# A Mamba block with a quantized feed-forward: the first sequence transposed and partly convolved on TensorE, and new places for the work at both ends

## The chip, the cores and the metric

The kernel runs on one core of a Trainium2 chip. The metric is device time in microseconds (us) of one execution; lower is better. The median of three runs of the kernel before is 1844.12 us (1842.97 to 1844.41).

A core has five engines, each with its own instruction queue worked off in order: PE (TensorE, matrix products), DVE (VectorE) and ACT (ScalarE) for elementwise work, POOL (GpSimd) for elementwise work too, and SP (SyncE), which here only issues DMAs. Engines wait for each other by semaphores. A waiting instruction holds up everything behind it in its own queue.

## The reference

Eight sequences of 2048 tokens with 256 features pass through a Mamba-like mixer and a feed-forward layer whose operands are rounded to FP4. Cut to what matters:

```
xz = x @ W_in;  x_proj, z = split(xz)          # 512 channels each
xc = causal_conv4(x_proj) + conv_b             # per channel, 4 taps
x_conv = silu(xc)
ssm = x_conv @ W_xproj                         # 1 + 16 + 16 columns
delta = softplus(ssm[0]);  Bm = ssm[1:17];  Cm = ssm[17:33]
h_mean = sum over the whole sequence of x_conv * (delta * Bm) / L
y = h_mean * Cm + D * x_conv
x = layernorm(x + (y * silu(z)) @ W_out)
g = fp4(x) @ fp4(w_gate).T;  u = fp4(x) @ fp4(w_up).T
x = layernorm(x + fp4(silu(g) * u) @ fp4(w_down).T)
```

`h_mean` is a sum over all tokens of a sequence: nothing after it can start for a sequence before its last token has passed the convolution and the softplus. `fp4` scales each block of 16 values by its maximum and rounds.

## The kernel before, in words

**Tiles.** A sequence is cut into 4 blocks of 512 tokens (32 blocks in all, named b0 to b31 here), and each block into 2 pairs of 256 tokens (64 pairs). The 512 channels are 4 chunks (c) of 128 partitions.

**Block, first half (`begin_block`, lines 575 to 754).** Channels lie on partitions, tokens along the row. Per chunk: `project` (PE, L602), `fetch` copies the result from PSUM (ACT, L611), `halo` copies the three last tokens of the block before (POOL, L595 and L597), `first` is the first tap (ACT, L616), three `tap`s follow (DVE, L622), then `silu` (ACT, L628). Then `x_projection` (PE, L635), `keep_ssm` (ACT, L645) and `by_token` (DVE, L650). To bring tokens onto the partitions, every chunk is `split` into 16-bit halves (ACT, L664), turned by a DMA transpose (issued by SP, L670) and put together again by `turned` (ACT, L678). `weigh` (DVE, L688) forms the delta column from it, `softplus` follows on DVE with one power on POOL (L502 to L526, L505), `delta_b` (DVE, L654) writes the tile `dB`, and `sums` (PE, L702) adds the block to the running sum. After a sequence's fourth block, `mean` (L712), `spread_mean` (L716) and `keep_mean` (L722) give `hT`.

**Block, second half (`mix_block`).** `state` (PE, L766) and `mix` (DVE, L777) form y, four blocks later (`LAG = 4`).

**Pair (`finish_pair`).** `zed` (PE, L810), `silu_z` (ACT, L821), `gated` (POOL, L826), `out` (PE, L833), `residual1` (DVE, L843), layernorm (DVE L545, POOL L551 to L556, ACT L559), the rounding q1 (DVE L289 to L328, ACT L320), whose result goes through a DMA transpose and is scaled by POOL (L392, tile `xqT`), `gate` and `up` (PE, L856), `silu_g` (ACT, L874), `product` (DVE, L881), the rounding q2 in the same way (tile `hqT`), `down` (PE, L887), `residual2` (DVE, L896), a second layernorm, `store`. The very last pair is worked in two halves of 128 tokens and transposes on PE (`finish_last`, L952 to L1043).

**Weights.** `w_gate`, `w_up` and `w_down` are rounded and transposed at the start in five portions (`prepare_...`): a load, the same rounding on DVE, ACT and POOL, transposes on PE (L451, L424, L487) and copies by ACT.

**The order of the work** is written out by hand. Every piece is put in a list with a place, a number; the list is sorted by it and the instructions are issued in that order, on each engine's queue:

```
    def at(base, table, name, index, f, *args):
        events.append((base + place, len(events), f, args))
```

For block n the base is n * 64, for its second half and its pairs (n + 4) * 64. The places come from the tables `BLOCK`, `PAIR`, `LAST` and `PREPARE`, the same for all blocks and pairs. Buffers come from rotating pools; PSUM has seven banks for all products and one for the running sum.

Of the kernel before, what the change touches and what calls it, by code (L numbers as in the profile page):

```python
# [8 lines left out]
F32 = mybir.dt.float32  # L9
BF16 = mybir.dt.bfloat16  # L10
U16 = mybir.dt.uint16
AF = mybir.ActivationFunctionType
ALU = mybir.AluOpType
# [3 lines left out]
P = 128  # L17
# [2 lines left out]

SIXTH = 0.16666668653488159
LN_EPS = 1e-5

# [2 lines left out]
PERIOD = 64.0  # L28
LAG = 4
BLOCK = {  # L30
    "load": -64.24,
    "halo": (-56.64, 17.17, 44.94, 44.05),
    "project": (-6.65, 11.59, 35.63, 20.08),
    "fetch": (1.54, 22.24, 57.11, 39.62),
    "first": (31.29, 32.95, 58.72, 51.03),
    "tap": ((35.31, 59.00, 62.56), (65.55, 67.78, 68.04), (72.08, 76.04, 76.92), (68.69, 69.87, 71.31)),
    "silu": (66.68, 70.49, 81.23, 75.04),
    "skip": (93.43, 94.37, 91.85, 154.42),
# [59 lines left out]
    "q1_gather_scales": (116.45, 146.97),  # L98
    "q2_gather_scales": (173.72, 195.66),
}  # L100
LAST = {
    "out": (101.01, 124.29),
    "residual1": (191.05, 124.61),
    "n1_stats": (194.16, 124.76),
    "n1_rstd": (197.81, 154.90),
    "n1_apply": ((198.21,), (173.78,)),
    "q1_scales": (212.63, 186.63),
    "q1_normalize": (212.96, 190.36),
    "q1_magnify": (213.66, 197.40),
    "q1_add": (229.95, 199.27),  # L110
    "q1_subtract": (370.03, 201.46),
    "q1_scale": (381.67, 203.71),
    "turn_xq": (512.71, 208.03),
    "turned_xq": (555.93, 212.80),
    "gate_up": ((593.00, 642.64, 617.68), (428.82, 267.08, 393.51)),
    "silu_g": ((596.51, 688.55, 679.34), (441.86, 473.75, 424.74)),
    "product": ((640.93, 768.07, 698.95), (535.88, 574.29, 531.93)),
    "q2_scales": (807.40, 593.68),
    "q2_normalize": (887.88, 627.15),
    "q2_magnify": (914.06, 635.31),  # L120
    "q2_add": (968.66, 643.81),
    "q2_subtract": (1012.32, 644.76),
    "q2_scale": (1095.84, 763.77),
    "turn_h": ((1144.78, 1139.10), (796.35, 946.12)),
    "turned_h": ((1205.14, 1146.35), (869.55, 1017.90)),
    "down": (1276.90, 1047.48),
    "residual2": (1296.41, 1121.36),
    "n2_stats": (1401.69, 1155.25),
    "n2_rstd": (1486.43, 1223.57),
    "n2_apply": ((1522.05,), (1243.96,)),  # L130
    "store": (1640.76, 1326.67),
}
PREPARE = {
    "weights": 27.56,
    "load": (-121.97, 130.79, 184.98, 271.53, 340.39),
    "scales": (-20.38, 135.83, 201.49, 277.18, 344.23),
    "normalize": (-15.59, 137.98, 203.68, 281.65, 345.11),
    "magnify": (17.95, 144.61, 207.82, 281.80, 360.53),
    "add": (31.07, 148.24, 209.79, 282.31, 368.84),
    "subtract": (96.60, 150.57, 211.47, 295.54, 376.69),  # L140
    "scale": (106.05, 151.39, 216.10, 314.72, 378.29),
    "turn": ((113.97,), (167.73, 177.76, 171.02), (249.86, 266.74, 247.22), (330.75, 339.14, 315.56, 339.84), (381.85, 389.94, 381.25, 386.21)),
}

@with_exitstack
def mamba_fp4_ffn_kernel(
# [16 lines left out]
    nc = tc.nc  # L163
    B, L, DM = x.shape
# [13 lines left out]
    NF = FF // P  # L178
    TAIL = FF - NF * P
    G = 32  # L180

    xf = x.rearrange("b (i t p) d -> b i p t d", p=P, t=NT)
    xTf = x_t.rearrange("b (k p) l -> b p k l", p=P)
# [41 lines left out]
    nc.vector.tensor_reduce(place, ident.rearrange("p (j n) -> p n j", n=G), AX.X, ALU.add)  # L225
    spread = const.tile([P, TT, G], F32, name="spread")
    nc.vector.tensor_copy(spread, place.unsqueeze(1).to_broadcast([P, TT, G]))
    nc.sync.dma_start(w_in_sb[:, :, :DI], w_in[:, :DI].rearrange("(k p) n -> p k n", p=P))

    xpool = ctx.enter_context(tc.tile_pool(name="xpool", bufs=2))  # L230
    keep = ctx.enter_context(tc.tile_pool(name="keep", bufs=LAG + 2))
# [2 lines left out]
    small = ctx.enter_context(tc.tile_pool(name="small", bufs=4))  # L234
    fp4 = ctx.enter_context(tc.tile_pool(name="fp4", bufs=2))

    def load_weights():
        nc.sync.dma_start(cw_sb, conv_w.rearrange("(c p) o k -> p c (o k)", p=P))
        nc.sync.dma_start(cb_sb, conv_b)
        wx = w_xproj.rearrange("(c p) n -> p c n", p=P)  # L240
        nc.sync.dma_start(w_xp_sb[:, :, :DS], wx[:, :, 1 + DS :])
        nc.sync.dma_start(w_xp_sb[:, :, DS:], wx[:, :, 1 : 1 + DS])
        nc.sync.dma_start(w_delta_sb, w_delta.to_broadcast([P, DI]))
        nc.sync.dma_start(w_in_sb[:, :, DI:], w_in[:, DI:].rearrange("(k p) n -> p k n", p=P))
        nc.sync.dma_start(dk_sb, d_skip)
        nc.sync.dma_start(w_out_sb, w_out.rearrange("(c p) n -> p c n", p=P))
# [3 lines left out]
    def at(base, table, name, index, f, *args):  # L250
        place = table[name]
        for i in index:
            place = place[i]
        events.append((base + place, len(events), f, args))

    def bank():
        return ps.tile([P, 512], F32, tag="ps", name="ps")
# [316 lines left out]

    def begin_block(n):

        b, i = divmod(n, NBLK)
        s = tiles["block", n] = {}

        def at_piece(name, f, *args):  # L580
            at(n * PERIOD, BLOCK, name, args, f, *args)

        def load():
            s["xT"] = xpool.tile([P, KM, T], F32, tag="xT", name="xT")
# [35 lines left out]
        def tap(c, k):  # L620
# [2 lines left out]
                acc, xp[:, k + 1 : k + 1 + T], cw_sb[:, c, k + 1 : k + 2], acc, ALU.mult, ALU.add  # L623
            )

        def silu(c):
            acc = s["xc"][:, c, :]
            nc.scalar.activation(acc, acc, AF.Silu, bias=cb_sb[:, c : c + 1])  # L628

        def x_projection():  # L630

# [15 lines left out]
        def by_token():  # L647

            s["ssm"] = p2.tile([P, P], F32, tag="ssm", name="ssm")
            nc.vector.transpose(s["ssm"], s["ct"])  # L650
            s["delta"] = small.tile([P, TT], F32, tag="delta", name="delta")

        def delta_b():
            nc.vector.tensor_tensor(  # L654
# [20 lines left out]
        def turned(c):  # L675
# [6 lines left out]
                s.pop(("hwT", c)).rearrange("p h t n -> p t n h"),  # L682
            )

        def weigh(t):
            if "d" not in s:
                s["d"] = small.tile([P, TT], F32, tag="d", name="d")
            nc.vector.scalar_tensor_tensor(  # L688
                p2.tile([P, DI], BF16, tag="xd", name="xd", bufs=1),
                s["xct"][:, t, :],  # L690
                1.0,
                w_delta_sb,
                ALU.mult,
                ALU.mult,
                accum_out=s["d"][:, t : t + 1],
            )

        def sums():
            if i == 0:
                hsum_of[b] = ps_h.tile([P, DI], F32, tag="h", name="hsum")  # L700
            for t in range(TT):
                nc.tensor.matmul(  # L702
                    hsum_of[b][t * G : (t + 1) * G, :],
                    dB_of[n % 2][:, t, :],
                    s["xct"][:, t, :],
                    start=(i == 0),
                    stop=(i == NBLK - 1),
                )
# [21 lines left out]
        for c in range(NC):  # L730
            at_piece("halo", halo, c)
            at_piece("project", project, c)
            at_piece("fetch", fetch, c)
            at_piece("first", first, c)
            for k in range(KC - 1):
                at_piece("tap", tap, c, k)
            at_piece("silu", silu, c)
            at_piece("skip", skip, c)
        at_piece("x_projection", x_projection)
        at_piece("keep_ssm", keep_ssm)  # L740
        at_piece("by_token", by_token)
        for c in range(NC):
            at_piece("split", split, c)
            at_piece("turn", turn, c)
            at_piece("turned", turned, c)
        for t in range(TT):
            at_piece("weigh", weigh, t)
        softplus(at_piece, lambda: s["d"], lambda: s["delta"])
        at_piece("delta_b", delta_b)
        at_piece("sums", sums)  # L750
        if i == NBLK - 1:
# [4 lines left out]
    def mix_block(n):  # L756

        b = n // NBLK
        s = tiles["block", n]

        def state():
            s["y"] = [bank().rearrange("p (c n) -> p c n", n=P) for _ in range(TT)]
            for c in range(NC):
                for t in range(TT):
                    g = slice(t * G, t * G + DS)
                    nc.tensor.matmul(  # L766
                        s["y"][t][:, c, :],
                        hT_of[b][g, c * P : (c + 1) * P],
                        s["ct"][g, :],
                        start=True,  # L770
                        stop=True,
                    )

        def mix(g):
            xc = s["xc"].rearrange("p c (t g r) -> p g c t r", g=TT, r=G)[:, g]
            y = s["y"][g].rearrange("p c (t r) -> p c t r", r=G)
            nc.vector.tensor_tensor(xc, xc, y, ALU.add)  # L777

        at((n + LAG) * PERIOD, BLOCK, "state", (), state)
        for t in range(TT):  # L780
            at((n + LAG) * PERIOD, BLOCK, "mix", (t,), mix, t)

    def finish_pair(m):

# [3 lines left out]
        s = tiles["block", n]  # L788
        q = {}

        def at_piece(name, f, *args):
            at((n + LAG) * PERIOD, PAIR, name, (half,) + args, f, *args)

        def stage(prefix):
            return lambda name, f, *args: at_piece(prefix + name, f, *args)
# [107 lines left out]
        for j in range(NC // 2):  # L903
            at_piece("zed", zed, j)
            at_piece("silu_z", silu_z, j)
            at_piece("gated", gated, j)
        if m == B * L // U - 1:
            for t in range(NT):
                finish_last(m, t, s, q)
            return  # L910
# [25 lines left out]
    def finish_last(m, t, s, pair):  # L936
# [129 lines left out]
        layernorm(stage("n2_"), x1, 1)  # L1066
        at_piece("store", store)

    at(0.0, PREPARE, "weights", (), load_weights)
    for n in range(B * NBLK):  # L1070
        begin_block(n)
# [61 lines left out]
```

## Time and profile before

| | |
|---|---|
| median of 3 runs | 1844.12 us |
| the profiled execution | 1842.3 us, span 1840.5 us |
| mean granted TensorE clock | 0.982 |
| PE busy | 1761.9 us (96% of the span) |
| DVE, ACT, POOL busy | 1551.0, 1021.5, 789.6 us |
| DMA | 203.62 MB, mean 111 GB/s |

The span is from the first to the last instruction; 1.8 us of the execution lie around it. "Busy" of PE counts the time in which a matmul runs. The granted clock is the share of full speed that the throttle gave TensorE. A float32 matmul leaves two records in the trace, a transpose by PE leaves one: a `project` (two matmuls) shows as four records.

A timeline row gives the start, the length, the engine, the line, the tiles and the count of a group of instructions, and in brackets the idle time of the engine before it with what ended that idle time. A row by stages gives the busy time (and count) of each engine in a stretch of the span, and the granted clock.

### The profile page before, as it was taken

What the parts mean: (1) busy time and instruction counts of PE and PEld (TensorE: products, weight loads), DVE (VectorE), ACT (ScalarE), POOL (GpSimd) and SP (SyncE); (2) the same over time, 40 slices, a digit from 0 to 9 for tenths busy, and PEclk for the clock granted to TensorE, in tenths of its full rate; (3) what the DMA queues carried; (4) which work ended last, traced back from release to release, by engine and by line L of the source; (5) the groups of instructions that cost most, each with busy time, mean ns of one, the idle gap of its engine ahead of it and who ended that gap; (6) DMA issues with size and microseconds to landing.
All of it is one profiled execution on the core that took longest, in us unless ns stands there. A gap on an engine that the chain in (4) does not pass through costs nothing.

```text
span 1840.5 us, 27813 instructions
## 1 busy us (share of the span) xinstructions
PE 1761.9 (96%) x9550; PEld 1407.9 (76%) x9550; DVE 1551.0 (84%) x3087; ACT 1021.5 (56%) x1554; POOL 789.6 (43%) x962
## 2 busy tenths in 40 slices
PE   5579999999999999999999999999999999999986
PEld 2246778888787888778788878788887878888874
DVE  4879989888888988888888888898888889877774
ACT  6886655556555555655555555555566556433222
POOL 1114353544434354453445444444444443455553
PEclk8799999999999999999999999999999999999997
DMA  4344664554555545555555555555455554444431
GB/s 128 89 102 90 118 124 110 114 124 104 121 121 112 118 115 121 104 122 121 112 115 120 114 108 125 122 113 118 116 112 114 121 114 103 121 106 102 99 85 27
DMA packets 383549, 203.62 MB, mean 111 GB/s; under 512 B 307120, under 2 KB 358192, under 8 KB 383408
## 3 DMA queue, kind: packets, MB, share of 16 engines
q1 hardware_dynamic: 383408, 201.85, 49.9%
q8 instruction: 75, 1.23, 0.3%
q14 instruction: 66, 0.54, 0.1%
HBM read 116.34 MB, written 20.91 MB: 75 GB/s over the span
## 4 chain that ended last, share of the span: by engine, by line
PE 87%; DVE 6%; issue 2%; POOL 2%; DMA 2%; ACT 1%; SPq 0%; POOLq 0%; DVEq 0%; ACTq 0%
PE ps L856 31%; PE ps L887 17%; PE ps L833 11%; PE ps L810 11%; PE ps L602 10%; PE ps L766 2%; PE hsum L702 2%; PE ps L635 1%; DVE xc L622 1%; DMA hwT<-hw 1%; DMA q_gT<-q_w 1%; DVE q_amax L289 1%; DMA xT<-in_x_t_dram 1%; POOL hqT L392 0%; DVE xd L688 0%
## 5 line engine op out<-in xcount | busy, mean ns | idle before, releaser
L887 PE MATMUL ps<-wdT,hqT 128*128 128x256 f32 x1512 | 342.4, 383 | 14.4 <-POOL hqT L392 14.4
L887 PEld LDWEIGHTS ps<-wdT,hqT 128*128 128x128 f32 x1512 | 286.9, 191 | 76.1 <-issue 22.6
L856 PE MATMUL ps<-wgT,xqT 128*128 128x256 f32 (+1 forms) x1512 | 328.6, 364 | 0.9 <-POOL xqT L392 0.9
L856 PE MATMUL ps<-wuT,xqT 128*128 128x256 f32 (+1 forms) x1512 | 320.2, 361 | 0.1
L856 PEld LDWEIGHTS ps<-wuT,xqT 128*128 128x128 f32 x1512 | 274.8, 190 | 50.2 <-issue 13.2
L856 PEld LDWEIGHTS ps<-wgT,xqT 128*128 128x128 f32 x1512 | 272.3, 190 | 45.7 <-issue 14.1
L826 POOL TENSOR_TENSOR xc<-xc,sz 128x512 f32<-128x512 f32 x128 | 162.6, 1281 | 298.5 <-DVE xc L777 263.7
L622 DVE SCALAR_TENSOR_TENSOR xc<-xp,cw_sb,xc 128x512 f32<-128x512 f32 x384 | 280.1, 750 | 5.8 <-ACT xc L616 1.7
L392 POOL TENSOR_TENSOR hqT<-q_gT,hqT 128x1408 f32<-128x1408 bf16 x63 | 185.6, 2947 | 207.2 <-PE ps L856 124.4
L821 ACT ACTIVATE sz<-ps 128x512 f32<-128x512 f32 x128 | 72.7, 595 | 335.3 <-PE ps L810 335.3
L602 PE MATMUL ps<-xT,w_in_sb 128*128 128x512 f32 x512 | 250.7, 616 | 8.5 <-DMA xT<-in_x_t_dram 8.5
L810 PE MATMUL ps<-xTz,w_in_sb 128*128 128x256 f32 x1024 | 241.8, 380 | 0.0
L833 PE MATMUL ps<-w_out_sb,xc 128*128 128x256 f32 x1008 | 231.0, 382 | 0.5 <-POOL xc L826 0.5
L810 PEld LDWEIGHTS ps<-xTz,w_in_sb 128*128 128x128 f32 x1024 | 195.3, 191 | 39.0 <-issue 13.8
L881 DVE TENSOR_TENSOR h<-sg,ps 128x512 f32<-128x512 f32 (+1 forms) x189 | 120.8, 640 | 116.0 <-PE ps L856 116.0
L874 ACT ACTIVATE sg<-ps 128x512 f32<-128x512 f32 x189 | 102.6, 560 | 203.6 <-PE ps L856 203.4
L833 PEld LDWEIGHTS ps<-w_out_sb,xc 128*128 128x128 f32 x1008 | 189.0, 190 | 31.3 <-POOL hqT L392 4.8
L320 ACT ACTIVATE q_w<-q_x 128x512 bf16<-128x512 f32 (+3 forms) x131 | 130.1, 993 | 94.5 <-DVE q_x L312 94.4
L324 DVE SCALAR_TENSOR_TENSOR q_x<-q_w,q_x 128x512 f32<-128x512 bf16 (+3 forms) x131 | 151.4, 1156 | 17.6 <-ACT q_w L320 15.0
L602 PEld LDWEIGHTS ps<-xT,w_in_sb 128*128 128x128 f32 x512 | 99.7, 199 | 86.6 <-issue 81.7
L559 ACT ACTIVATE x<-x,ln_nb,ln_rs 128x256 f32<-128x256 f32 x256 | 142.4, 595 | 31.4 <-POOL ln_nb L556 31.2
L328 DVE SCALAR_TENSOR_TENSOR q_w<-q_w,q_x 128x512 bf16<-128x512 bf16 (+3 forms) x131 | 151.6, 1158 | 2.4
(114 smaller groups left out, 2305.0 us busy)
## 6 DMA issues: line engine op xcount, KB each, us to landing
hqT<-q_rows SPq DMA_DIRECT2D x63, 704.0 KB
xT<-in_x_t_dram SPq DMA_DIRECT2D x32, 512.0 KB
xTz<-in_x_t_dram SPq DMA_DIRECT2D x64, 256.0 KB
xt<-in_L_attn_x_dram SPq DMA_DIRECT2D x64, 256.0 KB
xqT<-q_rows SPq DMA_DIRECT2D x63, 256.0 KB
out_dram<-x SPq DMA_DIRECT2D x63, 256.0 KB
q_rows<-q_scT SPq DMA_DIRECT2D x252, 4.0 KB
q_rows<-q_scT SPq DMA_DIRECT2D x252, 12.0 KB
```

The lines of the kernel that those rows point to most:

```text
L320: nc.scalar.activation(state["g"], state["x"], AF.Abs, scale=GRID)
L324: nc.vector.scalar_tensor_tensor(xn, w, 1.5 * GRID, xn, ALU.max, ALU.subtract)
L328: nc.vector.scalar_tensor_tensor(w, w, 1.5 * GRID, xn, ALU.max, ALU.subtract)
L392: nc.gpsimd.tensor_tensor(qT(), state["gT"], qT(), ALU.mult)
L559: nc.scalar.activation(r()[:, t, :], r()[:, t, :], AF.Identity, bias=v["nb"][:, t : t + 1], scale=v["rstd"][:, t : t + 1],)
L602: nc.tensor.matmul(mm, w_in_sb[:, k, c * P : (c + 1) * P], s["xT"][:, k, :], start=(k == 0), stop=(k == KM - 1),)
L622: nc.vector.scalar_tensor_tensor(acc, xp[:, k + 1 : k + 1 + T], cw_sb[:, c, k + 1 : k + 2], acc, ALU.mult, ALU.add)
L810: nc.tensor.matmul(q["mm", j][:, a, :], w_in_sb[:, k, DI + c * P : DI + (c + 1) * P], q["xT"][:, k, :], start=(k == 0), stop=(k == KM - 1),)
L826: nc.gpsimd.tensor_tensor(xc, xc, q["sz"][:, c, :], ALU.mult)
L833: nc.tensor.matmul(mm[:, t, :], s["xc"][:, c, o : o + P], w_out_sb[:, c, :], start=(c == 0), stop=(c == NC - 1),)
L856: nc.tensor.matmul(q[name, j][:, t, :n], q["xqT"][:, t * KM + k, :], wT[:, k, f0 : f0 + n], start=(k == 0), stop=(k == KM - 1),)
L887: nc.tensor.matmul(mm[:, t, :], q["hqT"][:, t * NF + j, :], wdT[t][:, j, :], start=(j == 0), stop=(j == NF),)
```

## The change

In the first sequence (blocks b0 to b3, `early`):

- The DMA transposes are replaced. `split`, `turn` and `turned` go; `turn_early` transposes on PE, per 128 tokens all four chunks into one PSUM bank (16 transposes per block); `weigh` reads that bank directly; `turned_early` copies the bank to SBUF (ACT, four copies per block) for `sums`.
- The fourth chunk's convolution moves from ACT and DVE to PE: `convolve` multiplies by four diagonal matrices and adds up in PSUM; `silu` reads the bank. POOL builds the diagonals once (`diagonals`).
- `w_in`'s first half is loaded in four pieces, and these, the convolution's weights and the diagonals have places in the list.

Everything in the first sequence's blocks is placed by a table of its own, `FIRST`. Pairs 0 and 1 are placed by `BEGIN`, pairs 61 and 62 by `END`, the state and mix of b31 and the shared part of pair 63 by `FINAL`; `LAST` and `PREPARE` have new numbers. `BLOCK` and `PAIR`, used by all the rest, are unchanged.

The core of the diff; most of the numbers in the tables are left out:

```
+FIRST = {
...
+    "turn": (79.93, 82.87, 83.29, 85.30),
+    "turned": (97.80, 89.40, 91.21, 107.43),
+    "sums": 122.29,
...
+    "weigh": (85.52, 89.72, 94.26, 90.27),
+    "convolve": (61.76,),
+}
+BEGIN = {
...
+END = {
...
+    "q2_turn": (346.34, 299.75),
+    "q2_scale": (349.76, 327.77),
+    "down": (370.81, 347.09),
...
+FINAL = {
+    "state": 64.63,
+    "mix": (68.48, 64.96, 73.47, 71.79),
...
 LAST = {
...
-    "gate_up": ((593.00, 642.64, 617.68), (428.82, 267.08, 393.51)),
+    "gate_up": ((268.99, 261.77, 255.72), (221.48, 214.39, 232.62)),
...
-    "down": (1276.90, 1047.48),
+    "down": (367.44, 314.17),
...
 PREPARE = {
-    "weights": 27.56,
...
+    "projection": (-22.19, -235.80, 12.21, -45.26),
+    "convolution": -7.30,
+    "diagonals": (46.75,),
 }
...
+    DIAG = 1
...
-    nc.sync.dma_start(w_in_sb[:, :, :DI], w_in[:, :DI].rearrange("(k p) n -> p k n", p=P))
...
+    def load_projection(c):
+        cols = slice(c * P, (c + 1) * P)
+        nc.sync.dma_start(w_in_sb[:, :, cols], w_in[:, cols].rearrange("(k p) n -> p k n", p=P))
...
+    def diagonals(c):
+        if not diag:
+            diag["w"] = p2.tile([P, NC, U], F32, tag="sz", name="diag").rearrange(
+                "p c (k n) -> p (c k) n", n=P
+            )
+        for k in range(KC):
+            nc.gpsimd.tensor_scalar(
+                diag["w"][:, c * KC + k, :], ident, cw_sb[:, NC - DIAG + c, k : k + 1], None, ALU.mult
+            )
...
+        early = n < NBLK
...
+            at(n * PERIOD, FIRST if early else BLOCK, name, args, f, *args)
...
+        def convolve(c):
+            mm = s["mm", NC - DIAG + c] = bank()
+            for k in range(KC):
+                nc.tensor.matmul(
+                    mm,
+                    diag["w"][:, c * KC + k, :],
+                    x_proj(NC - DIAG + c)[:, k : k + T],
+                    start=(k == 0),
+                    stop=(k == KC - 1),
+                )
...
-            nc.scalar.activation(acc, acc, AF.Silu, bias=cb_sb[:, c : c + 1])
+            nc.scalar.activation(acc, s.pop(("mm", c), acc), AF.Silu, bias=cb_sb[:, c : c + 1])
...
+        def turn_early(t):
+            tp = s["tp", t] = bank()
+            for c in range(NC):
+                nc.tensor.transpose(
+                    tp[:, c * P : (c + 1) * P], s["xc"][:, c, t * P : (t + 1) * P], ident
+                )
+
+        def turned_early(t):
+
+            if n % 2:
+                s["xct", t] = p2.tile(
+                    [P, DI], F32, tag="hw" if t < TT // 2 else "hwT", name="xct_early"
+                )
+            elif "xct" not in s:
+                s["xct"] = p2.tile([P, TT, DI], F32, tag="xct", name="xct", bufs=1)
+            nc.scalar.copy(by_channel(t), s["tp", t])
...
-                s["xct"][:, t, :],
+                s["tp", t] if early else s["xct"][:, t, :],
...
+        table = FIRST if n < NBLK else FINAL if n == B * NBLK - 1 else BLOCK
+        at((n + LAG) * PERIOD, table, "state", (), state)
...
+        table = FINAL if last else BEGIN if m < NT else END if m >= pairs - 3 else PAIR
...
+    for c in range(NC):
+        at(0.0, PREPARE, "projection", (c,), load_projection, c)
+    at(0.0, PREPARE, "convolution", (), load_convolution)
+    for c in range(DIAG):
+        at(0.0, PREPARE, "diagonals", (c,), diagonals, c)
```

## The prediction

> **What bounds the kernel now.** I read first the busy time of each engine by stages (start, length, then busy time with count for PE, weight loads, DVE, ACT, POOL; granted clock, DMA share, GB/s).
>
> ```profile
> 0.00:43.00 43.00, 22.41 (x69) 9.61 (x70) 18.04 (x47) 25.50 (x37) 4.65 (x25) 0.80 0.46 123
> 43.00:68.50 25.50, 13.75 (x68) 5.46 (x66) 20.71 (x45) 21.95 (x31) 5.03 (x7) 0.83 0.43 111
> 68.50:94.20 25.70, 15.82 (x62) 6.32 (x62) 20.80 (x44) 20.40 (x29) 4.77 (x5) 0.76 0.32 71
> 94.20:118.70 24.50, 20.26 (x95) 12.29 (x95) 19.23 (x44) 21.35 (x32) 3.59 (x8) 0.86 0.47 112
> 118.70:155.90 37.20, 31.17 (x184) 20.11 (x184) 31.97 (x69) 26.92 (x44) 12.61 (x18) 0.95 0.40 92
> 155.90:240.00 84.10, 83.40 (x482) 66.75 (x481) 78.31 (x156) 54.11 (x82) 37.11 (x47) 1.00 0.57 105
> 240.00:1737.40 1497.40, 1497.40 (x8245) 1221.07 (x8243) 1298.46 (x2574) 826.40 (x1260) 676.28 (x798) 1.00 0.52 115
> 1780.00:1840.50 60.50, 35.42 (x151) 28.76 (x149) 29.77 (x60) 13.93 (x28) 22.94 (x35) 0.84 0.13 36
> ```
>
> From 240 to 1780 us PE never rests at full clock. Its 78.6 us of idle time lie at the ends: 52.5 before the first gate (155.9), 25.1 after 1780. So the whole question is how early the first gate starts, what is added to PE meanwhile, and how long the end is. The first four stages are the blocks b0 to b3. What a block waits for is seen in the timeline around b1's end:
>
> ```profile
> 60.85 0.69 DVE L688 SCALAR_TENSOR_TENSOR xd<-xct,w_delta_sb 128x512 bf16<-128x512 f32 x1 [2.98 <-ACT xct L678]
> 65.58 0.17 DVE L509 TENSOR_SCALAR sp_u<-sp_e 128x4 f32<-128x4 f32 x1 [0.91 <-POOL sp_e L505]
> 68.25 0.22 DVE L654 TENSOR_TENSOR dB<-ssm,delta 128x64 f32<-128x64 f32 x1
> ```
>
> From `dB` to `dB` (43.06, 68.47, 94.19, 118.66) DVE works 20.7 of 25.4 us and waits 3.9, mostly for the DMA transposes (last `silu` 54.76, last turned chunk 60.8). The end is a chain of waits on PE:
>
> ```profile
> PE ps L635 <- ACT xc L628: 22.4, 6, 6.5
> PE ps L887 <- POOL hqT L392: 14.4, 2, 11.8
> PE ps L602 <- DMA xT<-in_x_t_dram: 8.5, 1, 8.5
> ...
> 1802.13 8.22 PE L887 MATMUL ps<-wdT,hqT 128*128 128x256 f32 x24 [11.84 <-POOL hqT L392]
> ```
>
> PE has done the gates of pair 62 by 1782.3, then waits 20 us for its rounding, and only afterwards starts the last pair.
>
> **The start.** The first product waits until 8.46 for `xT`, behind 512 KB of `w_in`, 128 KB of gate rows, and beside a second `xT`. Now 128 KB of `w_in` go ahead: 384 KB less, at 174 GB/s (mean of the first 20 us) 2.2 us. I take 6.5; bounds 5.5 and, if the four 128 KB pieces load no better, 8.5. Three more DMA issues on SP (0.47 each) push the convolution's weights by up to 1.4 us, covered by the first projection; uncovered, that is their cost.
>
> **What is added to PE.** A projection takes 1.71 us at full clock (110.38 to 112.09). The convolution is four matmuls of that form, 3.43 per block; 16 transposes at 0.115 (L424: ten in 1.15) are 1.84. Over four blocks: 21 us at full clock, 42 at half. It lies in idle time if clock and order allow.
>
> **Block b0.** The first 28 records took 14.20 us, seven projections with 2.1 us of slow clock; so five end at 6.5 + 2.1 + 8.6 = 17.2, the convolution at 20.6, b1's projection at 22.3. The last chunk fetched (0.58), first tap 0.72, three taps 2.2, `silu`: 23.0 with the table load of 1.28 and the three other `silu`s on ACT. Transposes from 23.0, `weigh` from 23.6. In the built order the second `weigh` waits for ACT's copy of the same bank; ACT has two weight copies, a first tap, a fetch and the copy ahead of it, some 3 us: 26.2. Three `weigh`s to 28.4, taps 2.2 over POOL's power, softplus, transpose, delta and `dB` 3.2: 34. Before: 43.06. **Gain 9.**
>
> **Blocks b1, b2.** 25.4, less three taps (2.2, they go to PE) and the waits of 3.9, is 19.3. A stall that goes makes the next thing late: turning needs `silu` 0.9 and four transposes 0.9 at half clock after the last tap, and DVE has 3.0 us of rounding there (L324, L328), so it is hidden; ACT's copies are the tight place. I add 1: 20.3, gain 5.1 each; bounds 2.2 (the waits return) and 6.1. Sixteen `split`s (1.04), sixteen `turned` (1.16) and the DMA transposes give way to sixteen copies of 0.58: ACT, 21 busy of 25, falls to about 15 per block and costs nothing.
>
> **Block b3.** 24.5, less the taps and waits of 2.15 (DMA `wdv`), 0.38, 0.85 and 0.82: 18. Gain 6.5. Each weight load on SP still stands behind the PE transposes that free its tile, and a block's `xT` behind it; `wv` issued at 61.58 was used at 74.98, now about 7 us after issue, against 7.8 for its predecessor, which DVE did not wait for. Uncovered: 1 to 3 us.
>
> **Diagonals.** Four POOL operations of 128x128 (0.29 the nearest, L342's 128x256 0.61): 1.2 to 2.4 us in POOL's idle 10.9, before 17.2. Nothing.
>
> So `sums` of b3 comes at 118.7 - 25.7 = 93. PE's work until `state` is then 75 us at full clock (21 projections 35.9, convolutions 13.7, transposes 7.4, weights 3.9, `zed` 5.2, the rest 8.9) in 86: it fits if the clock is mostly full.
>
> **From the mean to the first gate** the trace has 3.95 us to `state` (122.66) and 33.2 on to 155.90, a chain through mix, `gated`, `out`, layernorm, q1, transposes, POOL. The new order has the same chain; I count on DVE 11 taps 8.1, mixes 2.6, down-weights 4.4, `weigh` 3.1, two residuals with stats 3.9, q1 3.7, softplus 3.8, a wait for `out` of 4, then DMA 3.6 and POOL 1.5 to 2: some 34 after 1 of `state`. First gate at 131, **25 us earlier**. Bounds: 15 (cycles gain only the taps), 31 (start at 5.5, cycles of 19.3). PE's list after the gate holds the same work as before, and `BLOCK` and `PAIR` with it, so the 25 reach the end.
>
> **The end.** I align on the end of b31's `state` (1737.4). PE has 70.7 us of work left there, and the end comes 103.1 later: 32.4 lost. In the new order 79.3 us remain (one `down` and a half gate group with a `zed` more), without a wait until pair 62's gates are through at 52.5. The last pair's gates come next, in the former wait; then `down` of 61, the two small `down`s, and pair 62's `down` last. On DVE: pair 62's q2 starts 58.9, shares DVE with both halves of the last pair and ends at 75.4; DMA transpose 3.6, POOL 2.9 behind the last half: 81.9; PE is at 83 to 85 with the last half, `down` 5.2 (8.2 if slow) to 88 or 92; `residual2` and stats 1.9, POOL 1.5, ACT 1.1, store 2.9: 95.6 to 99.5. Lost 16.3 to 20.2: **gain 12 to 16, I take 13**. Bounds 5 (another 8 us chain like that at 1787 to 1795) and 17.
>
> **Sum.** 1842.3 - 25 - 13 = 1804.3 for an execution like the profiled one; the median lies 1.8 above that one: **1806**.
>
> **A rule that speaks against it.** After a PE wait of 6.5 us (56.54) projections run at 0.85 per record for some 4 us, then at 0.43; but after one of 2.05 us at 151.8, the eight records of L702 also took 1.94 us, where they take 1.06 elsewhere. The Trainium skill, "TensorE: Matmul & The Clock Gate", Part 1, puts the drop at an idle window of about 3.4 us. By that rule the new gaps of 2 to 3 us cost nothing; by the row each costs up to 2 us, mostly beside DVE's work. Its Part 4 says that transposes do not count as activity; then 16 of them in a row would drop the clock too. Ten transposes at 60.20 were followed by projections at full rate (four in 1.88), so the trace disagrees for ten. By the rule four blocks pay about 3.5 us each on PE, of which some 11 us are spare: 1809.
>
> **Rivals.**
> - The waits come back at another place: `weigh` behind ACT's copies or the turning in each block. For: ACT is in order and has 3 us ahead of the copy in b0. Against: from b1 on only a first tap and a fetch (1.3). Head 15: 1816.
> - The end gains little: pair 62 shares DVE with the last pair. Gain 5 or 0: 1814 to 1819.
> - The lead is given back after the first gate: DVE is 93% busy from 155.9 to 240, and if it, not PE, sets the pace, PE waits. Against: PE waited 0.7 us there. A loss of 10 to 36: 1816 to 1842.
> - Slower: PE becomes the bound of the head at half clock. 102 us of work stand before the first gate; with a slow share h it starts at 6.5 + 102(1+h) at best, later than 155.9 from h = 0.46. At h = 0.6 it is 170, 14 later; with 10 us of waits and the end's gain, 1855. For: the clock was 0.76 to 0.86 in these stages. Against: half speed follows waits, and such a PE would hardly wait.
> - The change does not do what it says: `xT` or the weights land late and b0 keeps its 43. Head 16: 1815, in the first rival's range.
>
> **How the numbers follow.** Forecast 0.55, own range 1796 to 1813; waits return 0.16; end gains little 0.11; given back 0.11, of which 0.02 wholly; slower 0.07. The range that leaves out 0.2 takes in the second and third cases and part of the fourth, and on the low side head 31 and end 17 (1796) with some of the slow clock that vanishes with the waits: 1790 to 1829. About 0.2% is what a measurement here tells from no change. Faster 0.91, same 0.02, slower 0.07.
>
> **What would show it.** Right: first product near 6.5; `dB` near 34, 54, 75, 92; no DVE wait over 1.5 us before `weigh`; `state` near 97; first gate near 131; PE without idle from there to about 52 us after b31's `state`; `down` of pair 62 as PE's last group. Wrong: a DVE wait on ACT before `weigh` in every block, projections at 0.85 per record in most of the head, PE idle between 160 and 240, or an end longer than 103 us after `state`.

## The result, and the profile after

The changed kernel takes 1797.18 us (median of four runs, 1796.08 to 1797.51), the kernel before 1843.55 us beside it: a ratio of 0.9748, interval 0.9731 to 0.9765. The profiled execution has a span of 1795.2 us at a mean granted clock of 0.995, 45.3 us under the 1840.5 of before. The forecast was 1806, with a range of 1796 to 1813; the time lies 1.2 us inside its lower end.

First the busy time of the engines by stages of the changed kernel (columns as before). The first four stages end with `dB` of b0 to b3, the fifth with the first gate product.

```profile
0.00:33.30 33.30, 24.24 (x94) 11.66 (x94) 16.48 (x46) 18.60 (x32) 9.53 (x30) 1.00 0.47 133
33.30:52.50 19.20, 17.70 (x90) 8.68 (x90) 18.19 (x42) 12.12 (x22) 5.31 (x6) 0.91 0.15 54
52.50:71.70 19.20, 16.93 (x92) 10.30 (x93) 18.20 (x42) 12.98 (x22) 4.67 (x5) 0.91 0.18 56
71.70:90.10 18.40, 18.40 (x102) 10.49 (x101) 14.31 (x40) 13.74 (x26) 3.39 (x8) 1.00 0.25 78
90.10:125.70 35.60, 33.10 (x198) 21.67 (x196) 31.19 (x71) 30.95 (x51) 15.21 (x21) 1.00 0.41 89
125.70:240.00 114.30, 114.30 (x650) 91.79 (x647) 107.10 (x203) 71.03 (x105) 44.76 (x54) 1.00 0.58 118
1750.00:1795.20 45.20, 32.08 (x139) 25.94 (x137) 28.85 (x49) 11.79 (x24) 15.22 (x23) 0.89 0.28 67
```

In the stages of b1 and b2 DVE now works 18.2 of 19.2 us, where it worked 20.7 of 25.5. PE, which worked 13.8 and 15.8 us there before, now works 17 to 18 of 19 us, and all of the next stage. From the first gate to 1750 us it has no idle time. The clock column of the first stage reads 1.00 although PE began slowly: its first 20 records, at 6.76, took 10.55 us, and 8.87 in a kernel of experiment 7. For the clock of a short stretch the length of the records is therefore the better witness.

The timeline of DVE around the end of b1 shows what became of the wait of 2.98 us before the first `weigh`:

```profile
44.25 0.68 DVE L879 SCALAR_TENSOR_TENSOR xd<-ps,w_delta_sb 128x512 bf16<-128x512 f32 x1
...
47.47 2.19 DVE L773 SCALAR_TENSOR_TENSOR xc<-xp,cw_sb,xc 128x512 f32<-128x512 f32 x3
49.58 0.16 DVE L655 TENSOR_SCALAR sp_u<-sp_e 128x4 f32<-128x4 f32 x1
...
52.30 0.23 DVE L822 TENSOR_TENSOR dB<-ssm,delta 128x64 f32<-128x64 f32 x1
```

No row has a bracket: neither `weigh` nor the step behind POOL's power (`sp_u`) waits. Three taps (at 47.47) stand in POOL's time.

The waits of PE over the whole kernel:

```profile
PE ps L753 <- DMA xT<-in_x_t_dram: 6.8, 1, 6.8
PE ps L1221 <- POOL last_h L488: 3.6, 2, 2.8
PE ps L862 <- ACT xc L792: 3.1, 3, 2.2
PE hsum L893 <- ACT xp L762: 2.1, 1, 2.1
...
PE ps L1089 <- POOL hqT L538: 0.2, 1, 0.2
```

The two rows that led the list before, 22.4 us on `silu` and 14.4 us on `hqT`, have become 3.1 and 0.2. And the end, from PE's timeline:

```profile
1775.52 1.54 PE L1221 MATMUL ps<-ident,last_h 128*128 128x128 f32 x6 [2.81 <-POOL last_h L488]
1776.99 5.19 PE L1232 MATMUL ps<-wdT,last_qT 128*128 128x256 f32 x12
1782.02 5.34 PE L1089 MATMUL ps<-wdT,hqT 128*128 128x256 f32 x24
```

`down` of pair 62 is now PE's last group. The 12 products ahead of it ran at half rate (5.19; the same twelve took 2.86 at 1769.85), behind a wait of 2.81 us.

**Where the 45.3 us come from.** The first gate starts at 125.70 instead of 155.90: 30.2. From the gate to the end of the span PE works 1656.4 us instead of 1658.5 (2.1) and rests 13.1 instead of 26.1 (13.0).

### The profile page after: what moved, and what is told of

Its sections match the earlier page's. It is cut to its first block, busy times and chain, and to the rows that moved or that the text cites. A ratio compares the mean times of both kernels' runs of the same rounds, so it can differ in the third digit from the quotient of the medians.

```text
span 1795.2 us, 27961 instructions
## 1 busy us (share of the span) xinstructions
PE 1766.7 (98%) x9646; PEld 1416.4 (79%) x9646; DVE 1539.8 (86%) x3075; ACT 993.8 (55%) x1534; POOL 793.4 (44%) x966
## 4 chain that ended last, share of the span: by engine, by line
PE 93%; DVE 4%; ACT 1%; issue 1%; POOL 1%; DMA 0%; SPq 0%; ACTq 0%; POOLq 0%; DVEq 0%
PE ps L1058 33%; PE ps L1089 18%; PE ps L1035 12%; PE ps L1012 12%; PE ps L753 11%; PE ps L963 2%; PE hsum L893 2%; PE ps L799 2%; DVE xc L773 1%; DVE q_amax L435 1%; PE ps L907 0%; DVE xd L879 0%; PE ps L862 0%; DVE q_w L474 0%; DVE q_x L458 0%
## 5 line engine op out<-in xcount | busy, mean ns | idle before, releaser
L773 DVE SCALAR_TENSOR_TENSOR xc<-xp,cw_sb,xc 128x512 f32<-128x512 f32 x372 | 270.2, 748 | 11.5 <-DMA dk_sb<-in_L_attn_D_dram 6.0
L753 PE MATMUL ps<-xT,w_in_sb 128*128 128x512 f32 x512 | 241.6, 597 | 6.8 <-DMA xT<-in_x_t_dram 6.8
L1012 PEld LDWEIGHTS ps<-xTz,w_in_sb 128*128 128x128 f32 x1024 | 194.3, 190 | 38.8 <-issue 13.8
L1076 ACT ACTIVATE sg<-ps 128x512 f32<-128x512 f32 (+1 forms) x189 | 102.6, 559 | 190.7 <-PE ps L1058 190.4
```

The costliest lines, as they stand in the source:

```text
L753: nc.tensor.matmul(mm, w_in_sb[:, k, c * P : (c + 1) * P], s["xT"][:, k, :], start=(k == 0), stop=(k == KM - 1),)
L773: nc.vector.scalar_tensor_tensor(acc, xp[:, k + 1 : k + 1 + T], cw_sb[:, c, k + 1 : k + 2], acc, ALU.mult, ALU.add)
L1012: nc.tensor.matmul(q["mm", j][:, a, :], w_in_sb[:, k, DI + c * P : DI + (c + 1) * P], q["xT"][:, k, :], start=(k == 0), stop=(k == KM - 1),)
```

## The experiments

All kernels compute the whole reference. Times are medians, with the kernel before at 1842.3 to 1844.1 beside them.

**1. Do the two ends add up?** The former places of the end in the changed kernel, and the new ones alone in the kernel before.

```
-        table = FINAL if last else BEGIN if m < NT else END if m >= pairs - 3 else PAIR
+        table = BEGIN if m < NT else PAIR
(and LAST, and state and mix of b31, as before)
```

> The changed kernel with the former places of pairs 61, 62, the last pair and b31's state. Theory (head and end add up, the end is worth what the alignment on b31's state gave): 13 to 14 us slower than the changed kernel, 1810 to 1811, with the 20 us wait of PE before the last pair back. Rival (the end gains little, the head gave nearly all 45 us): 1797 to 1802. The first gate stays at 125.7 in both.

> The kernel before with only the new places at the end. Theory: 13 to 14 us under 1843.6, so 1829 to 1831, first gate still at 155.9. Rival (the new end only works with the lead of the new start): no gain, 1843. If this run and the one with the former end disagree by more than 2 us, the two parts do not add up.

Measured: 1811.76 and 1827.97. Both lie about 1 us outside what was expected (1810 to 1811, and 1829 to 1831): the end is worth 14.6 us with the new start and 15.2 without it, where 13 to 14 were expected. The new start without the new end is worth 1843.13 - 1811.76 = 31.4; with 15.2 that is 46.6, against the 46.4 of the whole change (1843.55 - 1797.18). The parts add up, and the rival that the end gains little has fallen. In the kernel with the former end, PE's waits begin with the old row:

```profile
PE ps L1089 <- POOL hqT L538: 14.4, 2, 11.8
PE ps L753 <- DMA xT<-in_x_t_dram: 7.3, 1, 7.3
```

**2. The convolution on PE.** The fourth chunk goes back to ACT and DVE.

```
-    DIAG = 1
+    DIAG = 0
-    "first": (27.88, 18.67, 62.79),
+    "first": (27.88, 18.67, 62.79, 56.00),
-    "tap": (..., (74.79, 75.52, 77.67)),
+    "tap": (..., (74.79, 75.52, 77.67), (65.60, 66.20, 66.80)),
```

> The fourth chunk of the first sequence goes back to ACT and DVE: no diagonals, no convolution on PE, a first tap on ACT and three taps on DVE per block. Theory (DVE paces b0 to b3): 12 taps of 0.74 more on DVE, 8.9 us, block cycles of 21.4 instead of 19.2, 1806. Rival (PE's work decides, since PE rested only 15.2 us before the first gate): 13.7 us of PE work leave, so no loss, 1784 to 1798.

Measured: 1804.41 (1801.91 to 1805.64), 7.2 us more. PE lost 13.7 us of work and the kernel became slower, so PE's work does not set the pace of the start as a whole. DVE's timeline in that kernel:

```profile
33.62 0.22 DVE L822 TENSOR_TENSOR dB<-ssm,delta 128x64 f32<-128x64 f32 x1
...
55.05 0.22 DVE L822 TENSOR_TENSOR dB<-ssm,delta 128x64 f32<-128x64 f32 x1
...
76.48 0.22 DVE L822 TENSOR_TENSOR dB<-ssm,delta 128x64 f32<-128x64 f32 x1
...
95.15 0.22 DVE L822 TENSOR_TENSOR dB<-ssm,delta 128x64 f32<-128x64 f32 x1
```

The cycles of b1 and b2 are 21.43 us against 19.2: exactly three taps. b0 and b3 pay only 0.5 and 0.25, since DVE waited there anyhow (for `ps`, 2.06 us in b3) and the taps fill such waits. So `dB` of b3 comes 5.3 later, and the first gate, at 132.72, 7.0 later. The other 1.7 arise between the two on PE: it waits 2.42 us for `wdv` instead of 1.66, and what follows runs slower (six transposes 1.54 instead of 0.88, eight products 2.88 instead of 1.89). The theory holds for b1 and b2; its sum of 8.9 was too high because it charged all four blocks. The profiled execution, the fastest of the four, ends only 4.9 later, because its last 12 products took 2.86 instead of 5.19 behind the same wait.

**3. The order without the transposes on PE, and the transposes without the order.** First the changed kernel with `split`, DMA transpose and `turned` again; then the kernel before with `turn_early` and nothing else.

```
 FIRST (the first kernel)
-    "turn": (79.93, 82.87, 83.29, 85.30),
-    "turned": (97.80, 89.40, 91.21, 107.43),
+    "split": (66.90, 75.80, 77.80, 76.30),
+    "turn": (67.00, 75.90, 77.90, 76.40),
+    "turned": (78.00, 78.10, 78.30, 78.20),
```

> The first sequence's blocks are transposed by split, DMA transpose and turned copies again, each right behind its silu; all other places stay. Theory (the wait for the last turned chunk was a third of the loss): DVE waits some 3 us per block before the first weigh, 12 to 16 us in all, 1809 to 1813. Rival 1 (the new order alone hides the transposes): 1797 to 1799. Rival 2 (ACT, 12.1 to 13 us busy of 19.2 per block, takes 8.8 for splits and joins and gives up 2.3, and becomes the bound): cycles above 20 with ACT over 90% busy, and more than 1813.

```
+EARLY = dict(BLOCK, turn=(82.00, 82.10, 82.20, 82.30), turned=(86.50, 86.60, 86.70, 86.80))
(the second kernel: turn_early, turned_early and by_channel as in the change, for b0 to b3)
```

> The kernel before with the first sequence's blocks turned on PE, and nothing else: places, taps, loads and both ends as they were. Theory (the transposes alone bring back the wait for the last turned chunk, 2.98 of it in b1): no DVE wait before the first weigh, cycles of some 22.4 instead of 25.4, 9 to 12 us, 1831 to 1834. Rival 1 (in the former order the wait of DVE turns up at the transposes or at ACT's copies): 1839 to 1843. Rival 2 (the new places carry most of it): cycles as short as here do not show, and PE's waits on silu (22.4 us in four blocks) stay as they are; then the four blocks gain less than 12 us in all.

Measured: 1834.57 and 1847.3. Both expectations were wrong. With DMA transposes in the new order, DVE's timeline and SP's queue in b1 read:

```profile
64.40 0.69 DVE L880 SCALAR_TENSOR_TENSOR xd<-xct,w_delta_sb 128x512 bf16<-128x512 f32 x1 [7.58 <-ACT xct L847]
```

```profile
49.67 1.23 SPq L839 DMA_TRANSPOSE hwT<-hw  x1
51.00 0.53 SPq L737 DMA_DIRECT2D xT<-in_x_t_dram  x1
51.62 9.69 SPq L839 DMA_TRANSPOSE hwT<-hw  x3
```

`weigh` waits 7.58 us here and 39.6 over the four blocks, not 12 to 16. In this order all four chunks become ready within 7.4 us (the `silu`s run from 47.85 to 55.24), there are two `hw` tiles, and SP's last three transposes are issued over 9.7 us. ACT was busy 19.6 of 26.7 us, so rival 2's cause, a full ACT, is not it, though its time (more than 1813) came true. My places for these steps are not tuned ones; the run shows that this order needs a short way from `silu` to `weigh`, not that 37 us is the least that the DMA way costs.

The second kernel is slower than the kernel before: ratio 1.0024, interval 1.0015 to 1.0033. PE's timeline of its b1, and the row of DVE behind it:

```profile
44.89 0.38 PE L696 MATMUL ps<-ident,xc 128*128 128x128 f32 x2
52.77 3.25 PE L696 MATMUL ps<-ident,xc 128*128 128x128 f32 x14 [7.50 <-ACT xc L630]
55.81 2.10 PE L604 MATMUL ps<-xT,w_in_sb 128*128 128x512 f32 x4
57.84 1.08 PE L637 MATMUL ps<-xc,w_xp_sb 128*32 128x128 f32 x32
```

```profile
59.28 0.31 DVE L652 STREAM_TRANSPOSE ssm<-ct 128x128 f32<-128x128 f32 x1 [4.39 <-ACT ct L647]
```

The first two transposes are issued when two `silu`s are through; the third holds PE's queue for 7.5 us, with projections and `x_projection` behind it. `x_projection` comes late, then `keep_ssm`, and `by_token` (L652), which in the former order stands ahead of `weigh`, waits 4.39 us where `weigh` had waited 2.98. The cycle is 27.5 us instead of 25.4. That is rival 1, and worse than it. In `FIRST`, `by_token` stands behind the four `weigh`s and `x_projection` behind the transposes. Neither half pays alone: the first kernel, which has the new end, is 6.6 us slower than the new end with the old start (1827.97), the second 4 us slower than the kernel before.

**4. Work added to PE.** Every transpose is done twice.

```
-            for c in range(NC):
+            for c in 2 * list(range(NC)):
```

> Every transpose of the first sequence is done twice into the same place: 64 more, 7.4 us of PE at full clock. Theory (DVE paces the blocks): only what stands between silu and the first weigh shows, 0.46 per block, and the one wait of b3: 1 to 3 us, 1798 to 1800. Rival 1 (PE paces, since it is 88 to 100% busy in b1 to b3): the whole 7.4, 1804 to 1805. Rival 2 (transposes let the clock fall): projections at 0.85 per record behind 24 and more transposes, 1809 or more.

Measured: 1800.53, 3.4 more, between theory and rival 1. `dB` of b1 and b2 keeps its distances (19.2 and 19.4); b0 is 1.6 later, of which 0.6 is a later `xT` (7.34 instead of 6.76) and 0.6 slower first records (11.16 instead of 10.55), so that some 0.4 are left for the transposes. b3 has waits of 2.50 and 1.30 for `ps` and takes 20.2 instead of 18.4. The first gate is at 129.31, 3.6 later. So DVE paces b1 and b2, where it never waits, and PE paces b3, which the stage with PE at 18.40 of 18.40 already said; b0 is a chain in which DVE waits for PE (2.91) and ACT (1.57) in turn. Rival 2 fell:

```profile
43.85 3.50 PE L862 MATMUL ps<-ident,xc 128*128 128x128 f32 x30 [2.10 <-ACT xc L792]
47.27 1.08 PE L799 MATMUL ps<-xc,w_xp_sb 128*32 128x128 f32 x32
```

Thirty transposes in a row are followed by `x_projection` at its full rate of 1.08.

**5. The places of the first pairs.**

```
-        table = FINAL if last else BEGIN if m < NT else END if m >= pairs - 3 else PAIR
+        table = FINAL if last else END if m >= pairs - 3 else PAIR
```

> Pairs 0 and 1 get the places of all other pairs; everything else as in the changed kernel. Theory (the 29.7 us from the first state to the first gate, 33.2 before, come from these places): first gate 3 to 4 us later, 1800 to 1801. Rival 1 (they come from the work that is gone from this stretch): first gate at 126, 1797. Rival 2 (PE's order around the gates breaks): waits of PE after the first gate, more than 1803.

Measured: 1807.62 (1805.09 to 1809.58), 10.4 more. PE's timeline:

```profile
108.25 1.08 PE L799 MATMUL ps<-xc,w_xp_sb 128*32 128x128 f32 x16 [3.94 <-ACT xc L792]
...
134.60 3.04 PE L1058 MATMUL ps<-wgT,xqT 128*128 128x256 f32 x8 [3.00 <-POOL xqT L538]
```

The first gate comes at 134.60, 8.9 later. Of that, `dB` of b3 (91.04) is 0.9 later, with first records of 11.62 instead of 10.55; the places cost the other 8.0. From b3's `dB` to the gate it is 43.6 us here, 35.6 in the changed kernel and 37.2 in the kernel before. The common places among the new ones are worse than either full set, so the theory holds in kind (the stretch hangs on these places) and undersized them. The time of rival 2 (more than 1803) came true, but not its cause: the waits of 3.94 and 3.00 us lie before the first gate, not after it.

**6. The loads ahead of the first product.** `w_in`'s first half in one piece.

```
-        cols = slice(c * P, (c + 1) * P)
+        if c != 1:
+            return
+        cols = slice(0, DI)
```

> The changed kernel with the first half of w_in loaded in one piece of 512 KB at the place of the first 128 KB piece. Theory (384 KB at 174 GB/s stand ahead of xT): first product 2.2 us later, at 9, first gate and end 2 us later, 1799. Rival 1 (the three pieces and their issues cost as much as they save): first product at 6.8 to 7.3, 1797. Rival 2 (the late start is caught up, since DVE first works at 12): first product at 9, first gate as before, 1797.

Measured: 1798.18, 1.0 more. The first product starts at 8.13 (1.37 later), the first gate at 128.03 (2.3 later), but the span ends only 1.3 later. That lies between the theory (1799) and the two rivals (1797), and the clock blurs it. The first 20 records took 11.57 us instead of 10.55, which is the 1.0 that the gate is late beyond the first product; at the end, behind the same wait of 2.81, the six transposes and 12 products took 1.30 and 4.06 instead of 1.54 and 5.19, which gives 1.4 back. So 1.0 us is no clean price of the pieces. The wait before b0's sums, too, is 2.05 us in both kernels. PE's timeline there, of the kernel with one piece and then of the changed kernel:

```profile
35.87 1.07 PE L895 MATMUL hsum<-xct,dB 128*32 128x512 f32 x8 [2.05 <-ACT xp L764]
36.86 3.70 PE L782 MATMUL ps<-xp,diag 128*128 128x512 f32 x8
```

```profile
33.48 1.35 PE L893 MATMUL hsum<-xct,dB 128*32 128x512 f32 x8 [2.05 <-ACT xp L762]
34.76 5.07 PE L780 MATMUL ps<-xp,diag 128*128 128x512 f32 x8
```

The same wait is followed by full rate in the one and by a slow stretch in the other.

**7. Filling PE's waits.** Transposes (or products) of the identity, which nothing reads, in four waits; the excerpt is that at the last pair.

```
         def turn_h(i):
             q["tp", i] = bank()[:, : 3 * P].rearrange("p (j n) -> p j n", n=P)
+            if t == 0 and i == 0:
+                for _ in range(22):
+                    nc.tensor.transpose(q["tp", i][:, 0, :], ident, ident)
```

> Transposes of the identity, which nothing reads, stand in four of PE's waits: 24 before the first product, 18 before the first block's sums, 18 before the third chunk of b2 is turned, 22 before the second half of the last pair is turned. Theory (the clock falls after a wait of about 2 us, and any PE work holds it): the first seven projections lose 1.7 to 2 us less, the last 6 transposes and 12 products 2.8 us less; the two waits in the blocks lie beside DVE's work and bring nothing: 1792 to 1793. Rival 1 (the Trainium skill, "TensorE: Matmul & The Clock Gate", Part 4: transposes do not count as activity): no row gets faster, 1797 to 1798. Rival 2 (the same page, Part 1: the clock falls only after about 3.4 us): the filled waits of 2.05, 2.19 and 2.81 us change nothing, only the start can gain, 1795.

> The same four waits filled with half as many float32 products of the identity by itself (two records each). Theory: as with transposes, 1792 to 1793. Rival 1 (transposes do not count, products do): 1792 to 1793 here and 1797 to 1798 there. Rival 2 (a wait has to last 3.4 us): 1795.

Measured: 1792.46 with transposes, 1792.25 with products: 4.7 and 4.9 under the changed kernel, ratios to before 0.9726 (0.9712 to 0.9739) and 0.9727 (0.9713 to 0.974). PE's timeline with transposes:

```profile
1.61 5.38 PE L754 MATMUL ps<-ident 128*128 128x128 f32 x24 [1.61 <-POOL ident masks.py:199]
7.22 8.87 PE L756 MATMUL ps<-xT,w_in_sb 128*128 128x512 f32 x20 [0.23 <-DMA xT<-in_x_t_dram]
...
1770.66 2.56 PE L1230 MATMUL ps<-ident 128*128 128x128 f32 x22
1773.64 0.88 PE L1233 MATMUL ps<-ident,last_h 128*128 128x128 f32 x6 [0.42 <-POOL last_h L488]
1774.76 2.86 PE L1244 MATMUL ps<-wdT,last_qT 128*128 128x256 f32 x12 [0.24 <-ACT last_qT L1239]
1777.45 5.34 PE L1098 MATMUL ps<-wdT,hqT 128*128 128x256 f32 x24
```

The first 20 records of the projections take 8.87 instead of 10.55, the last 12 products 2.86 instead of 5.19. The first gate comes at 122.92 (2.8 earlier), the rest is 1.8 shorter. Useless work makes the kernel faster because it keeps the clock up. Both rivals fell: transposes serve as well as products, and a wait of 2.81 us, when filled, no longer slows what follows.

**8. The gate rows behind `xT`,** with 16 and then with 20 transposes at the start, the other waits filled as in 7.

```
-    "load": (-213.57, 90.49, 174.85, 253.57, 325.12),
-    "scales": (-75.36, 135.97, 197.54, 273.32, 339.85),
-    "normalize": (-35.43, 136.08, 201.57, 274.86, 340.86),
+    "load": (-30.00, 90.49, 174.85, 253.57, 325.12),
+    "scales": (-29.00, 135.97, 197.54, 273.32, 339.85),
+    "normalize": (-28.00, 136.08, 201.57, 274.86, 340.86),
```

> The kernel whose waits are filled with transposes (here 16 at the start), and the first gate and up rows are loaded behind xT and two pieces of w_in, with their first rounding steps. Theory (128 KB and two issues of SP, 0.57 and 0.58, leave the path to xT): first product at 5.8 to 6.2 instead of 7.2, 1 to 1.4 us in all, 1791. Rival (the rows now come late for DVE or ACT, and the first tap waits behind their rounding): first product earlier, first dB not, 1792 to 1793.

> The same as the kernel with the rows behind xT, but 20 transposes instead of 16 before the first product, so that they end at 6.1, where xT lands. Theory (the wait of 0.84 us between the 16 transposes and the first product made the warming up start again: 24 transposes with a gap of 0.23 were followed by full speed, 16 with a gap of 0.84 were not): first product at 6.1 to 6.3, the 20 records in 8.8 to 9.7 us, first dB at 31 to 31.6, 1791.2 to 1791.8. Rival (it is the length of the warming up, not the gap: 5.4 us were enough and 3.7 not, 4.5 are not either): the 20 records take 10.5 again and the time is that of the one with 16.

Measured: 1792.42 (1790.38 to 1793.04) and 1790.69 (1790.26 to 1790.95). PE's timeline of the first and of the second:

```profile
1.61 3.67 PE L754 MATMUL ps<-ident 128*128 128x128 f32 x16 [1.61 <-POOL ident masks.py:199]
6.12 10.77 PE L756 MATMUL ps<-xT,w_in_sb 128*128 128x512 f32 x20 [0.84 <-DMA xT<-in_x_t_dram]
```

```profile
1.61 3.73 PE L754 MATMUL ps<-ident 128*128 128x128 f32 x20 [1.61 <-POOL ident masks.py:199]
6.44 8.82 PE L756 MATMUL ps<-xT,w_in_sb 128*128 128x512 f32 x20 [1.10 <-DMA xT<-in_x_t_dram]
```

The first product comes about 1 us earlier, as expected. With 16 the rival's sign and time came true (first `dB` at 32.9, no earlier than the 32.1 of experiment 7), but through slow products, 10.77 instead of 8.87, and not through late rows. With 20 the first `dB` comes at 31.3. The reason that I gave for the slow start with 16 fell: with 20 the gap was longer, 1.10 us, and the products were at full rate. Nor is the rival right, since 3.73 us of dummy work were enough here, where 3.67 were not with 16. The 20 transposes took as long as the 16, so the full clock came during them. That the moment changes from run to run would fit the spread of 2.7 us with 16, but there is only one trace of each kernel. What decides it stays open. The kernel with 20 is the fastest of all: ratio to before 0.9712, interval 0.9699 to 0.9726, 6.5 us under the changed kernel.

## Why the prediction was right, and where it was off

- **The bound.** It named the start and the end as the only places where time can be had, and 43.2 of the 45.3 us came from there (30.2 and 13.0). Of the 20 us that it lets PE wait for the rounding of pair 62, 5.45 were `down` of pair 61; idle were 14.4.
- **The first product** came at 6.76 (forecast 6.5). The pieces are worth 1.37 us at the product, not the 2.2 of the sum, and 1.0 in all, in which the clock has its part (experiment 6).
- **b0** was forecast at 34 and ended at 33.33, with the second `weigh` waiting 1.57 us for ACT's copy, as worked out.
- **b1 and b2** were forecast at 20.3, b3 at 18; they took 19.2, 19.2 and 18.4. The step "I add 1" for turning was not needed: DVE waits nowhere in b1 and b2. The sign "no DVE wait over 1.5 us before `weigh`" held there, but not in b0 (2.47 and 1.57) and b3 (2.06). `dB` of b3 came at 90.1 instead of 92.
- **From the mean to the first gate** is the step that failed in size: the sum counted 39 us from b3's `dB` (92 to 131), and it took 35.6. That 39 was itself longer than the 37.2 of before, while "some 34 after 1 of `state`" against the former 33.2 hides it; the terms listed after it add up to about 39. The DVE part with its waits was 31.7 instead of 33.6 (the wait for `out` 2.2 instead of 4), and DMA transpose plus POOL 3.7 instead of 5.1 to 5.6. The text called it "the same chain"; experiment 5 shows that it hangs on the new places by 8.0 us. Nor is it DVE's chain alone any more: from 118.07 PE works without a wait up to the gate, and `xqT` was ready at 125.52, just before PE came to it at 125.70: the two ended together. So the start gave 30.2 at the gate, and 31.4 in experiment 1, where 25 were forecast; the first lies just inside the bounds of 15 to 31, the second just past them.
- **The end** was forecast at 13 (12 to 16). PE's rest after the gate fell by 13.0; exchanged as a whole, the end is worth 14.6 to 15.2. In the prediction's own alignment, b31's `state` ends at 1697.4 and the span 97.8 later, where 95.6 to 99.5 were forecast. `down` of pair 62 came last, as said.
- **What the sum left out:** 2.1 us less PE work behind the gate, of which slow products explain a part: in the profile before, `down` took 8.22 and a half `down` 4.37 behind waits, 4.4 us over the 5.34 and 2.86 of full rate; after, two groups lost 0.7 and 2.3.
- **The sum.** 38 forecast, 45.3 measured in the profiled executions: 5.2 from the gate, 2.1 from the work behind it. Both misses point the same way, so no larger errors cancelled; but the time is near the end of the range.
- **Diagonals:** forecast at 1.2 to 2.4 us for the four, measured 4.34. They ended at 17.48 while PE's convolution began at 17.14 on the first of them. It cost PE no wait, but the cover was all used, not ample.
- **Rivals.** The waits did not return and the lead was not given back (PE has no idle time between 125.7 and 240). PE at half clock was no bound: the clock column shows 0.91 in b1 and b2, and 1.00 in b0 and b3, where b0 lost 1.7 us on its first records. But PE has little room left: idle 1.5, 2.3 and 0 us in b1 to b3, and 7.4 us more cost 3.4 in experiment 4.
- **The rule weighed against the row.** In the Trainium skill, "TensorE: Matmul & The Clock Gate", Part 1 puts the drop at an idle window of about 3.4 us; here waits of 2.05, 2.19 and 2.81 us were each followed by slow work, and filling them ended it, so the measurement decides against it. That page of the Trainium skill also calls the window free-running, and the traces fit that: a wait of 2.05 slowed the changed kernel and not the one of experiment 6. No run shows the window itself. Part 4 of the same page of the Trainium skill, by which transposes do not count as activity, would have given 1809; experiments 4 and 7 disagree with it.

## What to carry to other kernels

Where one engine is full in the middle, ask when it becomes full and what it waits for at the end, and read those stretches one by one. A faster operation put into an order made for a slower one can lose: the transposes on PE alone cost 4 us, the new places and the rest of the change with DMA transposes kept only 9 of the 46 us (though their places were not tuned for it), and a step that waits early in an in-order queue is the first thing to look for. Where PE waits 2 us or more ahead of work that decides, unread products or transposes in the gap are worth a try: here they gave 4.7 us, and nothing that they compute is used.

## What the runs showed of the hardware

- The clock can fall after a PE wait of 2.05 us and stay up after one of the same length; transposes of the identity held and raised it as well as products did (1792.46 and 1792.25). Behind the same wait of 2.81 to 2.82 us at the end, the same 12 products took 5.19 us in the changed kernel, 4.06 in experiments 5 and 6, 3.69 in 4 and 2.86 in 2. So up to 2.3 us between two such kernels can be the clock's chance.
- Full clock came between some 3 and some 8 us after PE's first instruction: 24 transposes took 5.38 us in one run (0.224 each, all at half rate), 20 took 3.73 in another, which is 13 at 0.224 and 7 at 0.115. With 16 and then a gap of 0.84 us, the first five product records were still slow, until about 8 us.
- Four POOL products of a 128x128 tile with a column of scalars took 4.34 us, 1.08 each, where a POOL product of 128x256 (L488) took 0.62. Why was not tried.
